# Order of two eviction halves, and other slots for a few steps of the last layer, in a two-layer gated cross-attention kernel

## The chip, the core and the metric

The kernel runs on one core of one Trainium2 chip. The metric is the device time of one execution in microseconds (us). The engines are TensorE (PE in the profile; PEld is its weight load), VectorE (DVE), ScalarE (ACT), GpSimd (POOL) and SyncE (SP, which here only starts DMAs). TensorE writes its products to PSUM, a memory of eight banks here, each of 128 partitions by 512 fp32 numbers; VectorE and ScalarE read a product from its bank and write the result to SBUF, which is called evicting it.

## The reference

Four batches of 512 tokens of width 256 go through two layers, in fp32. Each layer is a cross-attention with 16 heads of width 16, whose keys and values come from the context, and a feed-forward part; each part gets a layer norm of x and is added back through a gate.

```python
x = x + tanh(g_xattn[0]) * attention0(layernorm(x), ctx)      # softmax(q k / 4 - 0.1 |t - t'|) v, then Wo, bo
x = x + tanh(g_ffn[0])   * ffn0(layernorm(x))                 # relu(x W1' + b1) W2' + b2, W' in {-1, 0, 1}
x = x + tanh(g_xattn[1]) * attention1(layernorm(x), ctx)      # q, k, v each through a relu; softmax(q k / 4) v
x = x + tanh(g_ffn[1])   * experts(layernorm(x))              # top-1 of 4 experts, gelu, Wo, bo, inner layer norm
```

In the first feed-forward part the weights are W / (mean |W|) rounded and cut to -1, 0 or 1; the hidden width is 1024 in both.

## The kernel before

**Groups and slots.** The attention of both layers is cut into 32 groups, in the order layer, batch b, half of the heads tt (0 or 1), and e (0 or 1). A projection of width 256 is two halves tt of 128 rows, on which eight heads lie; e tells the even heads from the odd. A group holds four heads, each on 32 partitions of which 16 carry data (the others are zero or hold helper rows). A group has four slots, one for each block of 128 keys (or, for the maxima, of 128 queries), which makes 128 slots u = 0 to 127: layer 0 is slots 0 to 63, layer 1 slots 64 to 127, and batch b of a layer begins at slot 64 * layer + 16 * b. So layer 1's batches 2 and 3 begin at slots 96 and 112.

**A slot.** Function `scores(u)` writes a block of eight matmuls, four heads twice: the scores `pm` of slot u + 6 (LEAD is 6), of which VectorE takes the row maxima (L521), and the transposed scores `psc` of slot u, of which ScalarE takes the exponentials (L536); they come as two groups of four, called quads here. The text calls this block S(u). After it `slot(u)` puts what else is due in that slot:

- `weighted`, in the first slot of a group: the sum `po` of the group before, 16 matmuls on its exponentials and values (L564), copied out by ScalarE (L570);
- `shifted`, in the third: the maxima of the next group transposed to `pmT` (L578) and subtracted from its queries, which makes `q2` (L587 where it is on POOL);
- `divided`, in the third (layer 1, and batch 0 of layer 0): `po` of the group before the last transposed to `pn` (L624), divided by its sums on VectorE and added to x on POOL (for the last group of batches 2 and 3 on VectorE);
- steps from the planner.

**The planner.** `chain(steps, start, end, *after)` takes steps that must follow one another, each with a cost in us and a gap: the step may come no sooner than that many slots after the one before it. A chain begins at slot `start`, after the chains named in `after`, and the last slot of each step is counted back from `end` by the gaps. In a slot the planner takes, among the chains' next steps, the one whose last slot is earliest, and takes it if it is due, if it costs 0, or if it fits in what is left of 3.1 (SLOT) by half its cost. Costs and gaps are the planner's numbers and no waits on the chip. The order in which the program writes instructions is their order on each engine[...].

**The steps that matter here.** `prepare(layer, b)` gives two lists. The first is the norm of the attention's input: `stats` and `more_stats` (each two of `BATCH_NORM_STATS2` and two of `BATCH_NORM_AGGREGATE` on VectorE, L335 and L336, and behind the second a chain of eight small POOL operations), `norm` (four rows on ScalarE, L366) and `turn` (eight transposes into two banks `pt_a`, copied to `xT` by ScalarE, or by ScalarE and VectorE, L382). The second is values: `values(0)` and `values(2)`, each two blocks of the value product `pv` (L430) in one bank. `project(layer, b, tt)` gives `keys` and `queries`: four matmuls (L461) into one bank `pk` or `pq`, and two evictions of that bank, one for each e. In layer 1 ScalarE evicts the half e = 0 (keys L476, queries L498) and VectorE the half e = 1 (L478, L500), and for values ScalarE the first block (L443) and VectorE the second (L445). In layer 0 the queries of batches 2 and 3 are shared in the same manner (L494 on ScalarE, L496 on VectorE); their keys are VectorE's alone (L474).

`ffn0(b)` gives the first feed-forward part of batch b: statistics, norm and transposes (`pt_f`), eight hidden products `ph` (L686) and two residual products `py_f` (L389, 32 matmuls each), which are added to x on VectorE (L394). `route(b)` gives the router's steps of the second (norm, transposes, logits `plg` and, per pair of tokens' blocks, the place of each token, `prk`, `pid`). `quantize` reads the absolute sums of the first feed-forward weights (L281, ScalarE) in the first slots.

**The banks.** All products share one pool: each new product gets the bank that comes free first in the order of the program. A matmul into a bank waits until all readers of what was there before have finished, and a second reader of a bank on another engine comes after the first one in the program.

The calls of the planner for the attention's steps, as they are before the change (L1169 to L1186), and the functions of the evictions follow.

Of the kernel before, what the change touches and what calls it, by code (L numbers as in the profile page):

```python
# [20 lines left out]
B, S, D = 4, 512, 256  # L21
# [20 lines left out]
LEAD = 6  # L42
# [10 lines left out]
def flamingo_kernel(ctx: ExitStack, tc: tile.TileContext, t: dict, out: bass.AP):  # L53
# [11 lines left out]
    def bank_psum(name):  # L65
        return ps.tile([P, 512], F32, tag="bank", name=name)
# [84 lines left out]
    def key_rows(tt, e, eng):  # L151
        kx = wts.tile([P, S], F32, tag="xg", name=f"kx{tt}{e}", bufs=4)
        beta = sml.tile([P, NT], F32, tag="beta", name=f"beta{tt}{e}")
        eng.tensor_scalar(beta, ext[:, e, 1, :], bqk[:, 1, tt, e : e + 1], None, ALU.add)
        for kt in range(NT):
            eng.tensor_scalar(
                kx[:, ts(kt, P)], kpos[:, ts(kt, P)], ext[:, e, 0, kt : kt + 1],
                beta[:, kt : kt + 1], ALU.mult, ALU.add,
            )
        kext[tt, e] = kx  # L160
# [63 lines left out]
    order = const.tile([P, NT, NE], F32, tag="order", name="order")  # L224
# [151 lines left out]
    def transposed(src, dst, name, alone=False):  # L376

        for c in range(NC):
            pt = bank_psum(f"pt_{name}{c}")
            for n in range(NT):  # L380
                nc.tensor.transpose(pt[:, ts(n, P)], src[:, n, ts(c, P)], ident)  # L381
            (nc.scalar.copy if alone or c == 0 else nc.vector.tensor_copy)(dst[:, c, :], pt)  # L382
# [18 lines left out]
    def prepare(layer, b, eng=None, meanwhile=None):  # L401

        nm = f"a{layer}_{b}"
        st = {}

        def stats():
            st["xn"] = act.tile([P, NT, D], F32, tag="xn", name=f"xn_{nm}")
            first, st["more"], st["rows"] = layernorm(
                x[b], st["xn"], 1e-5, nm, eng, meanwhile
            )  # L410
            first()

        def more_stats():
            st["more"]()

        def norm():
            st["rows"]()

        def turn():
            xTs[layer, b] = act.tile([P, NC, S], F32, tag="xT", name=f"xT_{nm}", bufs=2)  # L420
            transposed(st["xn"], xTs[layer, b], nm, layer == 0 and b > 0)

        def values(n0):
            def run():
                wv = attn_w[layer]["wv"]
                vh = v_sb[b % 2][1]
                pv = bank_psum(f"pv{nm}{n0}")
                for n in range(2):
                    for c in range(NC):
                        nc.tensor.matmul(  # L430
                            pv[:, ts(n, D)], lhsT=cT[b][:, c, ts(n0 + n, P)], rhs=wv[:, c, :],
                            start=(c == 0), stop=(c == NC - 1),
                        )
                if layer == 0:
                    nc.scalar.copy(
                        vh[:, n0 : n0 + 2, :, 0:DK], pv.rearrange("p (n h d) -> p n h d", n=2, d=DK)
                    )
                    return
                for n in range(2):
                    to = vh[:, n0 + n, :, 0:DK]  # L440
                    of = pv[:, ts(n, D)].rearrange("p (h d) -> p h d", d=DK)
                    if n == 0:
                        nc.scalar.activation(to, of, AF.Relu)  # L443
                    else:
                        nc.vector.tensor_scalar(to, of, 0.0, None, ALU.max)  # L445

            return run

        return (
            [(stats, 0, 0), (more_stats, 0, 1), (norm, 0, 1), (turn, 0.9, 1)],  # L450
            [(values(0), 1.75, 0), (values(2), 1.75, 0)],
        )

    def project(layer, b, tt):

        nm = f"{layer}_{b}{tt}"

        def product(w, src, name):
            pp = bank_psum(f"{name}{nm}")
            for c in range(NC):  # L460
                nc.tensor.matmul(  # L461
                    pp, lhsT=attn_w[layer][w][:, c, ts(tt, P)], rhs=src[:, c, :],
                    start=(c == 0), stop=(c == NC - 1),
                )
            return pp

        def key_half(pk, e):
            k = act.tile([P, S], F32, tag="k", name=f"k{nm}{e}", bufs=5)
            h = half[:, e : e + 1]
            if (layer, b) == (0, 1):  # L470
                nc.scalar.activation(k, pk, AF.Copy, scale=h)
                nc.gpsimd.tensor_tensor(k, k, kext[tt, e], ALU.add)
            elif layer == 0:
                nc.vector.scalar_tensor_tensor(k, pk, h, kext[tt, e], ALU.mult, ALU.add)  # L474
            elif e == 0:
                nc.scalar.activation(k, pk, AF.Relu, bias=kone[:, e : e + 1], scale=h)  # L476
            else:
                nc.vector.tensor_scalar(k, pk, h, kone[:, e : e + 1], ALU.mult, ALU.max)  # L478
            ks[layer, b, tt, e] = k

        def keys(between=None, halves=range(2)):
            pk = product("wk", cT[b], "pk")
            if between:
                between()
            for e in halves:
                key_half(pk, e)

        def queries():
            pq = product("wq", xTs[layer, b], "pq")
            for e in range(2):  # L490
                q = act.tile([P, S], F32, tag="q", name=f"q{nm}{e}", bufs=4)
                h = half[:, e : e + 1]
                if layer == 0 and (e == 0 or b < 2):
                    nc.scalar.activation(q, pq, AF.Identity, bias=bqk[:, 0, tt, e : e + 1], scale=h)  # L494
                elif layer == 0:
                    nc.vector.tensor_scalar(q, pq, h, bqk[:, 0, tt, e : e + 1], ALU.mult, ALU.add)  # L496
                elif e == 0:
                    nc.scalar.activation(q, pq, AF.Relu, scale=h)  # L498
                else:
                    nc.vector.tensor_scalar(q, pq, h, 0.0, ALU.mult, ALU.max)  # L500
                qs[layer, b, tt, e] = q

        return [(keys, 1.75, 1), (queries, 1.75, 0)]

    def score(out_, lhs, rhs, i, n):
# [640 lines left out]
    def chain(steps, start, end, *after):  # L1146
        last = [end] * len(steps)
        for i in range(len(steps) - 2, -1, -1):
            last[i] = last[i + 1] - max(steps[i + 1][2], 1 if steps[i][1] and steps[i + 1][1] else 0)
        c = dict(steps=list(zip(steps, last)), ready=start, after=after, done=None)  # L1150
        chains.append(c)
        return c

    def first_unit(layer, b):
        return 4 * NT * (B * layer + b)

    ffn = head = None
    ffns = []
    for b in range(B):
        first, rest = ffn0(b)  # L1160
        end = first_unit(1, b) - 15
        head = chain(first, 4 * NT * (b + 1) + 3, 4 * NT * (b + 1) + 9, head)
        ffn = chain(rest, 0, end, head, ffn)
        ffns.append(ffn)
    for layer in range(2):
        for b in range(B):
            u0 = first_unit(layer, b)
            lead, values = prepare(layer, b)
            if (layer, b) == (0, 1):  # L1169
                *early, early_rows, turn_1 = (job for job, *_ in lead)  # L1170
                (early_values, *_), later_values = values
                turned_1 = chain([later_values, (turn_1, 0.9, 1)], 1, 4)
                keys_0, (queries_0, cost, _) = project(layer, b, 0)
                chain([keys_0, (queries_0, cost, 2)], 5, u0 - LEAD - 2, turned_1)
            elif u0:
                chain(
                    [*lead, *project(layer, b, 0)], u0 - 14, u0 - LEAD - 2,
                    ffns[b] if layer else None,
                )
                chain(values, u0 - 8, u0 + 2)  # L1180
            if (layer, b) == (0, 1):
                keys_1, (queries_1, cost, _) = project(layer, b, 1)
                chain([keys_1, (queries_1, cost, 4)], u0 - 5, u0)
            else:
                chain(project(layer, b, 1), max(u0 - 4, 0), u0)
    (totals1, *_), *quant1 = quantize(w1f, "w1", True)  # L1186
# [14 lines left out]
    for b in range(B - 1):  # L1201
        u0 = first_unit(1, b + 1)
# [60 lines left out]
    lead, values = prepare(0, 0, nc.vector, lambda: key_rows(0, 0, nc.vector))  # L1263
    keys, queries = project(0, 0, 0)
# [119 lines left out]
    first = LISTS[2][1]  # L1384
# [131 lines left out]
```

## Time and profile before

| | us |
|---|---|
| median of 3 runs (lowest, highest) | 829.17 (829.14, 830.67) |
| the profiled execution's own time | 829.16 |
| its span, first to last instruction | 827.4 |
| what lies around the span | 1.76 |
| mean granted TensorE clock | 0.997 |

The times and the span are of one core. In the profile a row of instructions names the line, the engine, the operation, output <- input, and the shape; `x512 | 317.0, 682` means 512 instructions, 317.0 us busy in all, 682 ns for one; then comes the engine's idle time just before them and which instruction ended most of it. In the view of waits, a row such as `DVE k L478 <- ACT k L476: 10.0, 8, 1.7` means that VectorE waited at L478 for ScalarE's L476, 10.0 us in all, 8 times, 1.7 us at most. A row of the timeline begins with the start and the duration in us.

A mark for the stages is the start of `po`, which stands in every fourth slot. In the profiled execution the stages between such marks are busy as follows:

| from po of slot | to po of slot | length | PE | DVE | ACT | POOL |
|---|---|---|---|---|---|---|
| (start) | 4 | 50.07 | 45.04 | 38.71 | 24.23 | 27.92 |
| 4 | 24 | 88.66 | 88.43 | 65.63 | 57.94 | 56.34 |
| 24 | 60 | 207.70 | 207.69 | 141.91 | 102.13 | 75.54 |
| 60 | 88 | 157.06 | 156.90 | 108.33 | 86.28 | 32.55 |
| 88 | 112 | 127.00 | 125.21 | 86.56 | 68.55 | 20.28 |
| 112 | (700 us) | 69.51 | 68.53 | 41.65 | 46.87 | 24.73 |
| (700 us) | (end) | 127.40 | 116.67 | 80.77 | 46.39 | 57.69 |

A matmul that waits counts as busy here from the time its engine takes it up, so that PE is shown busy nearly always; how long a block takes from its start to the next one's start tells more. The marks within the fifth stage are po of slot 88 at 503.49, 92 at 528.68, 96 at 556.17, 100 at 571.82, 104 at 592.38, 108 at 610.91 and 112 at 630.49.

### The profile page before, as it was taken

How to read it: one execution, taken by the hardware profiler on the slowest of the kernel's cores; microseconds unless marked ns; L12 is line 12 of the kernel's file. 1: busy time of each engine (PE TensorE's matmuls, PEld its weight loads, DVE VectorE, ACT ScalarE, POOL GpSimd, SP SyncE). 2: the span in 40 equal slices, each digit the busy share in tenths (PEclk: the TensorE clock that was granted, in tenths of full speed). 3: DMA queues.
4: the chain of work that ended last, by engine and by line, in shares of the span. 5: the costliest groups of instructions: out<-in, count | busy, mean ns of one | idle time of the engine just before them, and what ended most of it. 6: DMA issues, size and time to landing. Idle time of an engine off the chain costs nothing. (4 is left out here: it accounts for less than half of the span.)

```text
span 827.4 us, 13610 instructions
## 1 busy us (share of the span) xinstructions
PE 808.5 (98%) x5226; PEld 451.6 (55%) x5226; DVE 563.6 (68%) x1254; ACT 432.4 (52%) x904; POOL 295.0 (36%) x457
## 2 busy tenths in 40 slices
PE   7999999999999999999999999999999999999995
PEld 3544444545464355643465444564444555899994
DVE  6867778766857676567855676557688764799443
ACT  2586665643645453455535566346756666533341
POOL 5658555524233253331011132002314421735622
PEclk9999999999999999999999999999999999999998
DMA  8200000000001000000000001000104322726820
GB/s 316 75 1 1 1 2 1 1 1 1 1 1 39 1 1 1 1 27 1 1 1 1 27 1 52 1 1 1 52 1 153 95 87 78 286 75 245 304 81 32
DMA packets 17712, 42.28 MB, mean 51 GB/s; under 512 B 2032, under 2 KB 12016, under 8 KB 15216
## 3 DMA queue, kind: packets, MB, share of 16 engines
q0 software_dynamic: 5104, 27.34, 9.3%
q1 hardware_dynamic: 12128, 13.54, 4.8%
q8 instruction: 41, 0.67, 0.3%
q10 hardware_dynamic: 416, 0.54, 0.2%
q14 instruction: 23, 0.19, 0.1%
HBM read 35.13 MB, written 6.29 MB: 50 GB/s over the span
## 5 line engine op out<-in xcount | busy, mean ns | idle before, releaser
L521 DVE TENSOR_REDUCE m<-pm 128x1 f32<-128x512 f32 x512 | 317.0, 682 | 109.6 <-PE psc L507 105.2
L536 ACT ACTIVATE p<-psc 128x512 f32<-128x512 f32 x512 | 266.9, 602 | 144.9 <-PE psc L507 142.8
L507 PE MATMUL psc<-q,k 32*128 32x512 f32 x1024 | 274.7, 622 | 0.0
L507 PE MATMUL pm<-k,q 32*128 32x512 f32 x1024 | 261.0, 615 | 1.7 <-ACT q L494 0.9
L539 POOL TENSOR_TENSOR p<-p,dec 128x256 f32<-128x256 f32 x128 | 93.9, 739 | 162.8 <-ACT p L536 162.8
L507 PEld LDWEIGHTS pm<-k,q 32*128 32x128 f32 x1024 | 91.9, 184 | 81.9 <-issue 45.8
L507 PEld LDWEIGHTS psc<-q,k 32*128 32x128 f32 x1024 | 106.0, 183 | 51.7 <-issue 27.4
L564 PE MATMUL po<-p,v 128*32 128x512 f32 x1024 | 116.5, 595 | 0.8 <-DVE m L521 0.8
L564 PEld LDWEIGHTS po<-p,v 128*32 128x32 f32 x1024 | 31.4, 109 | 80.9 <-issue 58.9
L1108 PE MATMUL pg<-xs,wg 128*128 128x128 f32 x608 | 71.6, 276 | 0.7 <-DVE m L521 0.7
L1108 PEld LDWEIGHTS pg<-xs,wg 128*128 128x128 f32 x608 | 69.8, 192 | 4.1 <-DVE m L521 1.7
L587 POOL TENSOR_TENSOR q<-q,mT 128x512 f32<-128x512 f32 x16 | 20.3, 1270 | 132.3 <-ACT mT L586 132.3
L1134 ACT ACTIVATE ha<-pg,wg 128x128 f32<-128x128 f32 x120 | 34.3, 368 | 52.5 <-PE pg L1108 52.5
L686 PE MATMUL ph<-xTf,w1q 128*128 128x512 f32 x128 | 60.0, 605 | 0.0
L570 ACT COPY oT<-po 128x512 f32<-128x512 f32 x32 | 18.7, 585 | 77.0 <-PE po L564 77.0
L1311 PE MATMUL pyf<-wo,ha 128*128 128x256 f32 x256 | 57.6, 379 | 0.0
L389 PE MATMUL py_f<-w2q,h 128*128 128x256 f32 x256 | 57.2, 381 | 0.0
L389 PEld LDWEIGHTS py_f<-w2q,h 128*128 128x128 f32 x256 | 48.0, 190 | 9.3 <-DVE m L521 3.0
L1311 PEld LDWEIGHTS pyf<-wo,ha 128*128 128x128 f32 x256 | 47.6, 190 | 5.9
L686 PEld LDWEIGHTS ph<-xTf,w1q 128*128 128x128 f32 x128 | 22.6, 189 | 30.3 <-issue 18.2
L394 DVE SCALAR_TENSOR_TENSOR x<-py_f,tg,x 128x512 f32<-128x512 f32 x8 | 6.0, 750 | 42.4 <-PE py_f L389 42.4
L461 PE MATMUL pk<-cT,wk 128*128 128x512 f32 x68 | 33.5, 615 | 0.3 <-DMA cT<-in_ctxT_dram 0.3
(263 smaller groups left out, 839.8 us busy)
## 6 DMA issues: line engine op xcount, KB each, us to landing
x<-in_x_dram SPq DMA_DIRECT2D x4, 512.0 KB, 8.4
rows_d<-xn_f SPq DMA_DIRECT2D x4, 512.0 KB, 3.0
rows_d<-x SPq DMA_DIRECT2D x4, 512.0 KB, 3.4
cT<-in_ctxT_dram SPq DMA_DIRECT2D x3, 512.0 KB, 9.5
w1q<-in_w_dram SPq DMA_DIRECT2D x1, 1024.0 KB, 8.9
w2q<-in_w_dram SPq DMA_DIRECT2D x1, 1024.0 KB, 11.2
wo<-in_wo_dram SPq DMA_DIRECT2D x2, 512.0 KB, 3.8
rows<-in_rows_dram SPq DMA_DIRECT2D x1, 640.0 KB, 9.1
```

Of the source, the lines that this page charges most:

```text
L389: nc.tensor.matmul(py[:, n, :], lhsT=operand(c, n0 + n), rhs=w[:, c, :], start=(c == 0), stop=(c == chunks - 1),)
L461: nc.tensor.matmul(pp, lhsT=attn_w[layer][w][:, c, ts(tt, P)], rhs=src[:, c, :], start=(c == 0), stop=(c == NC - 1),)
L507: nc.tensor.matmul(out_, lhsT=lhs[r, ts(n, P)], rhs=rhs[r, :], start=True, stop=True)
L521: nc.vector.tensor_reduce(m[:, n, 2 * pair + i, r : r + 1], pm[i], AX.X, ALU.max)
L536: nc.scalar.activation(p[:, i, :], psc[i], AF.Exp, scale=SCALE)
L539: nc.gpsimd.tensor_tensor(d, d, dec.unsqueeze(1).to_broadcast([P, 2, P]), ALU.mult)
L564: nc.tensor.matmul(po[i * HP : (i + 1) * HP, :], lhsT=v_sb[b % 2][0][:, kt, c0 : c0 + HP], rhs=ps_exp[NT * s + kt, i // 2][:, i % 2, :], s ...
L587: nc.gpsimd.tensor_tensor(q2s[g], qs[g], turned, ALU.subtract)
L686: nc.tensor.matmul(ph, lhsT=w1q[:, c, ts(f, P)], rhs=st["xT"][:, c, :], start=(c == 0), stop=(c == NC - 1),)
L1108: nc.tensor.matmul(ph[:, f, :], lhsT=w[:, c, ts(f2 * NF // 2 + f, P)], rhs=xs[j][:, c, :], start=(c == 0), stop=(c == NC - 1),)
L1134: nc.scalar.activation(ha[:, f, :], (ha if src is None else src)[:, f, :], AF.Gelu, bias=biases[j][:, fa : fa + 1],)
L1311: nc.tensor.matmul(py, lhsT=hs[j, f // 4][:, f % 4, :], rhs=wo1[f // 4][:, f % 4, :], start=(f == 0), stop=(f == NF - 1),)
```

## The change

It has four parts.

1. **The order of two evictions of one bank.** The value halves of layer 1 are written with VectorE's block first, then ScalarE's. The key and query halves are written with e = 1 (VectorE's) first in layer 1 and for batches 2 and 3 of layer 0; batches 0 and 1 of layer 0 keep e = 0 first. Nothing is moved to another engine.
2. **`turn_1`**, the second transposes of batch 1's input in layer 0, has a gap of 2 instead of 1 behind the values ahead of it.
3. **The last layer's last batch**: the first feed-forward part of batch 3 is due two slots earlier (slot 95, not 97); both statistics steps stand in slot 96 (16 before the batch begins), the rest of that chain from slot 97, and its first queries two slots behind its keys, not in the slot they could come in next. The chain of the three outer batches is as before.
4. **Gaps in layer 1**: the second values of batch 2 come six slots or more behind the first; the second queries (tt = 1) of batches 2 and 3 two slots or more behind their keys.

```diff
-                for n in range(2):
+                for n in (1, 0):
                     to = vh[:, n0 + n, :, 0:DK]
                     of = pv[:, ts(n, D)].rearrange("p (h d) -> p h d", d=DK)
...
+        order = (1, 0) if layer == 1 or b > 1 else (0, 1)
+
-        def keys(between=None, halves=range(2)):
+        def keys(between=None, halves=order):
             pk = product("wk", cT[b], "pk")
...
-            for e in range(2):
+            for e in order:
                 q = act.tile([P, S], F32, tag="q", name=f"q{nm}{e}", bufs=4)
...
-        end = first_unit(1, b) - 15
+        end = first_unit(1, b) - (17 if b == B - 1 else 15)
...
-                turned_1 = chain([later_values, (turn_1, 0.9, 1)], 1, 4)
+                turned_1 = chain([later_values, (turn_1, 0.9, 2)], 1, 4)
...
             elif u0:
-                chain(
-                    [*lead, *project(layer, b, 0)], u0 - 14, u0 - LEAD - 2,
-                    ffns[b] if layer else None,
-                )
-                chain(values, u0 - 8, u0 + 2)
+                if (layer, b) == (1, B - 1):
+
+                    (first, *_), (second, *_), *rest = lead
+                    norm = chain([(first, 0, 0), (second, 0, 0)], u0 - 16, u0 - 16, ffns[b])
+                    keys_0, (queries_0, cost, _) = project(layer, b, 0)
+                    chain([*rest, keys_0, (queries_0, cost, 2)], u0 - 15, u0 - LEAD - 2, norm)
+                else:
+                    chain(
+                        [*lead, *project(layer, b, 0)], u0 - 14, u0 - LEAD - 2,
+                        ffns[b] if layer else None,
+                    )
+                if (layer, b) == (1, 2):
+                    values_0, (values_2, cost, _) = values
+                    chain([values_0, (values_2, cost, 6)], u0 - 8, u0 + 2)
+                else:
+                    chain(values, u0 - 8, u0 + 2)
...
+            elif layer == 1 and b > 1:
+                keys_1, (queries_1, cost, _) = project(layer, b, 1)
+                chain([keys_1, (queries_1, cost, 2)], u0 - 4, u0)
             else:
                 chain(project(layer, b, 1), max(u0 - 4, 0), u0)
```

Since the planner fills slots one after the other, steps that the diff doesn't name move as well. In the program as it is built, these are the steps that TensorE has in other slots (the other slots keep theirs):

| slot | before | after |
|---|---|---|
| 2 | pmT, pt_a | pmT |
| 3 | | pt_a |
| 90 | pmT, pn, plg, ph | pmT, pn, pv(0), plg |
| 91 | prk, py_f | ph, prk |
| 93 | pk, pq | py_f |
| 94 | pmT, pn, py_f | pmT, pn, pk |
| 95 | pv(0), pv(2) | py_f |
| 96 | po | po, pq |
| 97 | | pv(2) |
| 98 | pmT, pn | pmT, pn, pt_a |
| 99 | | pk |
| 101 | pt_a | pq |
| 102 | pmT, pn, pk | pmT, pn |
| 103 | pq, pt_f | pt_f |
| 109 | pk, pq | pk |
| 111 | pid | pq, pid |

The order of SyncE's instructions is the same. On POOL the eight small operations of batch 3's norm stand ahead of the query shift and of the addition to x of slot 98.

## The prediction

> **What bounds the kernel now.** I read the page first: its engine totals, then its groups.
>
> ```profile
> PE 808.5 (98%) x5226; PEld 451.6 (55%) x5226; DVE 563.6 (68%) x1254; ACT 432.4 (52%) x904; POOL 295.0 (36%) x457
> ...
> L521 DVE TENSOR_REDUCE m<-pm 128x1 f32<-128x512 f32 x512 | 317.0, 682 | 109.6 <-PE psc L507 105.2
> L536 ACT ACTIVATE p<-psc 128x512 f32<-128x512 f32 x512 | 266.9, 602 | 144.9 <-PE psc L507 142.8
> ```
>
> TensorE (PE) is busy nearly always, and VectorE (DVE) and ScalarE (ACT) wait for its scores (psc). So a step is worth only what it does to PE's order in time. In the timeline of PE a score block S(u) (eight matmuls of slot u) takes 1.93 us from its start to the next block's when nothing holds it; longer ones hold a stall. From the weighted sum po of slot 88 (503.49 us) to that of slot 112 (630.49) the pieces at their shortest sum to 114.5 us (24.3 to slot 92, 56.5 to 104, 17.1 to 108, 16.6 to 112), so 12.5 of the 127.0 us are stall. All that most of the diff can win lies here.
>
> Next the waits, for the evictions whose order is turned round:
>
> ```profile
> DVE k L478 <- ACT k L476: 10.0, 8, 1.7
> DVE v L445 <- ACT v L443: 7.0, 7, 1.4
> DVE q L500 <- ACT q L498: 5.7, 6, 1.5
> PEld psc L507 <- DVE q L500: 3.1, 6, 0.6
> ```
>
> VectorE waits 22.7 us for ScalarE's half, and PE waits for the later half. One such place in the timeline, slots 93 and 94:
>
> ```profile
> 536.21 0.78 ACT L476 ACTIVATE k<-pk,kone,cols 128x512 f32<-128x512 f32 x1 [0.64 <-PE pk L461]
> 537.02 0.81 DVE L478 TENSOR_SCALAR k<-pk,cols,kone 128x512 f32<-128x512 f32 x1 [1.12 <-ACT k L476]
> ...
> 537.92 0.69 ACT L498 ACTIVATE q<-pq,cols 128x512 f32<-128x512 f32 x1 [0.94 <-PE pq L461]
> ...
> 538.71 0.75 DVE L500 TENSOR_SCALAR q<-pq,cols 128x512 f32<-128x512 f32 x1 [0.89 <-ACT q L498]
> ...
> 539.52 1.12 PE L507 MATMUL psc<-q,k 32*128 32x512 f32 x2
> ```
>
> The last pair of S(94) reuses pq's bank: it starts 0.05 us after the second reader ends, and the next block 1.05 later. S(94) takes 2.76 us, 0.83 over.
>
> **The order of the two halves.** Either way the second half starts when the first ends: 0.69 + 0.75 is 0.75 + 0.69. Here a rule of the Trainium skill is weighed (PSUM — Partial Sum Buffer, section PSUM bank collisions raise a hardware error): two engines must not touch one bank at a time, reads included, so a dependency stands between them. The rows above agree, back to back with 0.04 to 0.10 us between. Were the reads free of each other, each of the nine or so blocks that wait for the second half would gain some 0.7, 6 us in all; by row and rule it is 0. The handover from DVE to ACT no row shows; I bound it by 0.1 us either way for each such block (1 us in all), and take 0, as the opposite handover is that short.
>
> The gain is that DVE is free 0.7 earlier, and the cost that ACT's exponentials start some 0.3 later (2.06 for four, 539.12 becoming 539.4). Both are hidden where a long PE piece (po 3.57, py_f 7.1) follows, which is nearly everywhere. Where DVE is late, though, ACT used to read first in its shadow. That is so in layer 0, slots 24 and 40, where four statistics rows stand ahead of DVE's query half:
>
> ```profile
> 226.09 0.81 DVE L496 TENSOR_SCALAR q<-pq,cols,bqk 128x512 f32<-128x512 f32 x1
> ...
> 226.95 1.12 PE L507 MATMUL psc<-q,k 32*128 32x512 f32 x2
> 228.00 1.07 PE L564 MATMUL po<-p,v 128*32 128x512 f32 x8
> ```
>
> In slot 40 the built program now gives that pair a bank that the block's first reduction (0.62) frees: 226.8 + 0.62, so it starts at 227.45, +0.5. In slot 24 it waits for ACT's half after DVE's: 136.5 + 0.75 + 0.75 = 138.05 against 137.38, of which 0.3 was a wait of po for a reduction anyway: +0.35. In slot 79 DVE reaches its value half at 455.25, and ACT's 0.38 comes after: +0.2. Slots 30, 46, 87 and 88 gain about 0.1 each. In slot 107 the +0.4 hides behind DVE's rank of slot 108. **Sum +0.7.**
>
> **turn_1 from slot 2 to slot 3.** The transposes (1.0) leave the place before S(3) and go behind it. But ACT's order matters:
>
> ```profile
> 45.89 1.11 ACT L382 COPY xT_a<-pt_a 128x512 f32<-128x512 f32 x2
> ...
> 48.77 0.71 ACT L281 ACTIVATE abs_w<-w2q 128x512 f32<-128x512 f32 x1
> ```
>
> The copies now stand behind S(3)'s exponentials (46.0 to 48.0) and both absolute sums of slot 3 (1.25): 49.2 to 50.3. S(4)'s third score reuses the bank of the first copy, so it starts at 49.8 and po at 50.85 against 50.07. **+0.8.** If the copies were not waited for, S(4) would end by 49.4: -0.7.
>
> **Slots 88 to 104** (times from po of slot 88; in brackets before). Moved: values(0) 95 to 90, values(2) 95 to 97, the last hidden product 90 to 91, outputs 91 to 93 and 94 to 95, key product 93 to 94, query product 93 to 96; for batch 3 statistics 99 to 96, normalising 100 to 97, transposes 101 to 98, keys 102 to 99, queries 103 to 101. No matmul is added, SP's order is the same, and no DMA is moved; POOL's eight small steps (571.27 to 574.22, 2.95 us) come before the query shift of slot 98, which waits for its copy till later.
> To 92: S(91) is 1.93 (2.77), as the query bank is gone from it; ph waits 0.35 for a reduction, S(92) 0.37 for the rank. PE work 24.3 - 7.08 + 1.83 = 19.05, so po(92) 19.8 (25.19).
> To 96: po 3.57, S 1.93, py_f 7.08, S 1.96, transposes 1.0, pk 1.81, S(95) 2.75 (its last pair waits for k 0.8 and one reduction), py_f 7.0, S 1.96: 29.06, po(96) 48.86 (52.68). With po and pq 5.39 PE is at 54.25, call it T.
> To 100 from T: S(97) 2.55 (waits for q, 0.75 + 0.69), pva 1.83. DVE does q, all four statistics (2.16, by these rows) and only then its reductions, 2.9 to 5.35:
>
> ```profile
> 566.58 0.41 DVE L335 BATCH_NORM_STATS2 st_a<-x 128x6 f32<-128x256 f32 x1
> 567.03 0.18 DVE L336 BATCH_NORM_AGGREGATE mv_a<-st_a 128x2 f32<-128x6 f32 x1
> ...
> 568.37 1.13 PE L507 MATMUL pm<-k,q 32*128 32x512 f32 x4 [0.47 <-DVE m L521]
> ...
> 571.82 0.64 PE L564 MATMUL po<-p,v 128*32 128x512 f32 x4 [0.52 <-DVE m L521]
> ```
>
> v ends on DVE at 5.75, on ACT at 6.2; S(98) waits for it, 4.4 to 7.15. Behind v ACT stands the normalising of batch 3 (ready from POOL at 5.95; 2.07, to 8.27), and behind that S(98)'s exponentials. pt_a needs the bank of their first: 8.85 instead of 8.15, and ends at 9.85. S(99) waits for their last and then for the copies, 2.6, to 12.45; pk 1.82; S(100) 2.58. po(100) at T + 16.85 = 71.1 (68.33).
> To 104: po 3.57, S 1.93, pq 1.82, S(102) 2.58 (q's chain), transposes 1.1, S(103) 2.65 (late reductions behind the other batch's statistics), pt_f 1.45 (normalising to 14.4), S(104) 2.95 (copies behind late exponentials): 18.05 (20.56), po(104) 89.15 (88.89). The stall of the light slots isn't filled: each work put there brings its own eviction. **+0.3**; the two ends of the unknown are below, with the rivals.
>
> **Slots 109 to 112.** The query product goes from 109 to 111. S(110) starts 1.8 earlier, waits for ACT's k (620.08) and ends at 621.15; DVE's selections (1.28 and 0.5) follow its k at 619.26, reductions 620.95 to 623.4; pmT, pn, pidT to 622.8; S(111) waits for the division, to 625.4; pq to 627.2, pid, S(112) waits for q, to 629.9 against 630.49. **-0.6.**
>
> The end of batch 3's chain, the gap in the last layer's second value product and the two-step start of the norm change no more than these moves: 0.
>
> **Sum:** 0.7 + 0.8 + 0.3 - 0.6 = +1.2. Span 827.4 + 1.2 = 828.6; the profiled execution's 829.16 (1.76 around its span, the median of the runs being 829.17) becomes **830.3 us**. I call a difference of 0.2% (1.7 us) what a measurement of this kernel can tell.
>
> **Rival A, ScalarE becomes the bound (slower).** In slots 97 to 104 the normalising stands ahead of exponentials twice, after a POOL chain that starts late. I charge 0.7 and about 1 for them. If POOL's 2.95 or the statistics run later, the whole 2.07 of ACT goes on the path: 2 x 2.07 - 1.7 = +2.4 more, of which 2.0 stays: 832.3. It decides once xn of batch 3 ends later than T + 8.3. For it: ACT has no slack behind v. Against: ACT is 52% busy.
> **Rival B, the light slots are filled (faster).** S(97) to S(100) hold 3.3 us of stall and S(102) to S(104) 2.3. My 89.15 for slots 88 to 104 holds 8.4 of stall over the 80.8 of PE work. If the evictions fit in DVE's idle time and only 5.0 of it is there, the stretch gives -3.1 instead of +0.3: 826.9. For it: DVE is only 68% busy. Against: the rows of slot 99, where PE waits for DVE itself.
> **Rival C, the halves matter more.** If DVE's earlier 0.7 is worth 0.3 in each of eight blocks, -2.4: 827.9; the heavy pieces after them speak against it.
>
> **How the numbers follow.** Forecast 0.42 (829.0 to 831.4 by itself: 0.02 faster, 0.29 same, 0.11 slower): it follows the waits one by one. B 0.25 (0.22 faster, 0.03 same): stalls that I add up one behind the other may overlap. A 0.18 (0.02 same, 0.16 slower); C 0.15 (0.10 faster, 0.05 same). Faster 0.34, same 0.39, slower 0.27. The range takes in A and 0.3 beyond it, and B and 0.9 beyond, since B and a third of C (0.8) can hold together: 826.0 to 832.6.
>
> **What will show it.** po(92), po(96), po(100), po(104), po(112) minus po(88): 19.8, 48.9, 71.1, 89.2, some 126.7. DVE's wait for ACT's k, q and v gone, and ACT waiting for DVE's with S(62), S(72) and S(78) as long as before. po of slot 4 at 50.85; po of slot 40 0.5 later within its own slot. It would be wrong if PE's score blocks in slots 97 to 104 are near 1.93 (B), or if exponentials of slots 98 and 103 start later than I say (A).

## The result and the profile after

The changed kernel takes 831.13 us (median of 15 runs, 831.03 to 833.32) against 829.14 for the kernel before (15 runs): a ratio of 1.0028, interval 1.0021 to 1.0035. It is slower by 2.0 us. The forecast was 830.3, with 826.0 to 832.6 as range.

The profiled execution of the changed kernel took 831.66, with a span of 830.0. Single executions of one kernel differ by a step of about 0.6 or 1.6 us, in the profiles mostly in the first 20 us: `po` of slot 4 starts at 50.07 in the profile of before, at 49.42 in one and at 51.72 in two profiles of kernels with the same code up to there. So what follows compares marks inside the executions, each against the mark ahead of it, and not totals. Summed in this manner the change costs 2.5 us up to `po` of slot 128 in the execution that was profiled, 0.5 more than the medians say. The likely reason is such a step: the changed kernel's times lie at 831.1, 831.7 and 833.3 us, most of them at the first, those of before at 828.5, 829.1 and 830.7, most of them at the second. Matched in this order they differ by 2.5 to 2.7. No execution at 831.1 was profiled, so this is not shown.

The page of the changed kernel, first part and the two groups shown of before:

```profile
PE 812.1 (98%) x5226; PEld 450.1 (54%) x5226; DVE 565.3 (68%) x1254; ACT 429.4 (52%) x904; POOL 294.9 (36%) x457
...
L524 DVE TENSOR_REDUCE m<-pm 128x1 f32<-128x512 f32 x512 | 317.2, 682 | 116.1 <-PE psc L510 112.9
L539 ACT ACTIVATE p<-psc 128x512 f32<-128x512 f32 x512 | 265.4, 602 | 130.9 <-PE psc L510 129.4
```

No instruction is added, and no engine is busier by more than 4 us; VectorE's idle time ahead of the maxima grows from 109.6 to 116.1 us, nearly all of it spent waiting for scores. The waits of the evictions (waiting instruction, releaser, us in all, times, longest) have changed sides:

```profile
ACT v L443 <- DVE v L445: 15.2, 8, 2.8
ACT q L497 <- DVE q L499: 14.1, 4, 3.8
ACT k L476 <- DVE k L478: 12.3, 8, 2.6
ACT q L501 <- DVE q L503: 9.2, 8, 2.2
PEld psc L510 <- ACT q L501: 3.4, 7, 0.6
```

In the rows shown of before VectorE waited 22.7 us for ScalarE's half of keys, values and queries of the last layer; now ScalarE waits 50.8 us for VectorE's, 14.1 of them (L497) for queries of layer 0. Both sums are whole idle times, and part of them passed before the product was there. They alone say nothing about the end: TensorE waits for the second half, whoever reads it (for queries of the last layer 3.1 us in the fourth row of the prediction's waits, 3.4 in the last row here).

Where the time went, by the start of `po` (us against before; "forecast" is the prediction's own term):

| stretch | before | after | difference | forecast |
|---|---|---|---|---|
| to slot 4 (turn_1) | 50.07 | 50.78 | +0.71 | +0.8 |
| slots 20 to 24 (halves, layer 0) | 21.46 | 21.81 | +0.36 | +0.35 |
| slots 36 to 40 (halves, layer 0) | 21.15 | 21.60 | +0.44 | +0.5 |
| other slots up to 88 (halves) | | | -0.07 | -0.2 |
| 88 to 92 | 25.19 | 19.64 | -5.55 | -5.4 |
| 92 to 96 | 27.49 | 29.78 | +2.29 | +1.6 |
| 96 to 100 | 15.65 | 22.57 | +6.93 | +6.6 |
| 100 to 104 | 20.56 | 18.08 | -2.48 | -2.5 |
| 104 to 112 | 38.11 | 37.73 | -0.38 | -0.6 |
| 112 to 128 | 65.55 | 65.83 | +0.28 | 0 |

Three of these places in the timeline (start, duration, instruction). Slot 40: VectorE reaches its query half at 227.16, behind the statistics, and ScalarE, idle for 3.84 us, reads only after it. The block's last pair doesn't wait for that read, which ends at 228.75, but for the bank of VectorE's first maximum, which VectorE can take only behind its half, as forecast.

```profile
227.16 0.78 DVE L499 TENSOR_SCALAR q<-pq,cols,bqk 128x512 f32<-128x512 f32 x1
...
227.97 0.78 ACT L497 ACTIVATE q<-pq,bqk,cols 128x512 f32<-128x512 f32 x1 [3.84 <-DVE q L499]
...
228.59 1.12 PE L510 MATMUL psc<-q,k 32*128 32x512 f32 x2 [0.23 <-DVE m L524]
229.64 0.64 PE L567 MATMUL po<-p,v 128*32 128x512 f32 x4
```

Slots 3 and 4: the two copies of turn_1 stand on ScalarE behind the exponentials and the absolute sums, and half of the next block's transposed scores wait for the first copy's bank.

```profile
49.02 1.13 ACT L382 COPY xT_a<-pt_a 128x512 f32<-128x512 f32 x2
...
49.72 1.13 PE L510 MATMUL psc<-q,k 32*128 32x512 f32 x4 [0.17 <-ACT xT_a L382]
50.78 1.50 PE L567 MATMUL po<-p,v 128*32 128x512 f32 x12
```

Slot 95, the largest miss: VectorE is in the division of the group before (`o`) when the key product is ready, reads it at 542.72, and ScalarE after that. The block S(95) takes 3.23 us where 2.75 were forecast.

```profile
542.38 0.42 DVE L637 TENSOR_TENSOR o<-pn,rec 128x256 f32<-128x256 f32 x1
...
542.72 0.80 DVE L478 TENSOR_SCALAR k<-pk,cols,kone 128x512 f32<-128x512 f32 x1
...
543.55 0.78 ACT L476 ACTIVATE k<-pk,kone,cols 128x512 f32<-128x512 f32 x1 [2.58 <-DVE k L478]
...
545.22 1.13 PE L389 MATMUL py_f<-w2q,h 128*128 128x256 f32 x4
```

### The profile page after: what moved, and what is told of

The parts are those of the page before. It is cut to its first block, busy times and chain, and to the rows that moved or that the text cites. A ratio compares the mean times of both kernels' runs of the same rounds, so it can differ in the third digit from the quotient of the medians.

```text
span 830.0 us, 13609 instructions
## 1 busy us (share of the span) xinstructions
PE 812.1 (98%) x5226; PEld 450.1 (54%) x5226; DVE 565.3 (68%) x1254; ACT 429.4 (52%) x904; POOL 294.9 (36%) x457
## 5 line engine op out<-in xcount | busy, mean ns | idle before, releaser
L524 DVE TENSOR_REDUCE m<-pm 128x1 f32<-128x512 f32 x512 | 317.2, 682 | 116.1 <-PE psc L510 112.9
L510 PE MATMUL psc<-q,k 32*128 32x512 f32 x1024 | 279.1, 622 | 1.0 <-ACT q L497 0.4
```

Source lines behind the costliest of these rows:

```text
L510: nc.tensor.matmul(out_, lhsT=lhs[r, ts(n, P)], rhs=rhs[r, :], start=True, stop=True)
L524: nc.vector.tensor_reduce(m[:, n, 2 * pair + i, r : r + 1], pm[i], AX.X, ALU.max)
```

## The experiments

### The parts by themselves

First the order of the halves alone, on the kernel before:

```diff
-                for n in range(2):
+                for n in (1, 0):
...
+        order = (1, 0) if layer == 1 or b > 1 else (0, 1)
-        def keys(between=None, halves=range(2)):
+        def keys(between=None, halves=order):
...
-            for e in range(2):
+            for e in order:
```

> The kernel before with only the order of the halves turned round (keys, queries and values in layer 1, queries in batches 2 and 3 of layer 0); every step stays in its slot. Theory: the loss is layer 0's alone, where VectorE is late behind the statistics: po of slot 24 +0.36, slot 32 +0.12, slot 40 +0.44, slot 48 +0.11, then -0.3 in layer 1 to slot 88, and nothing in slots 88 to 128: +0.7, 829.9 us. Rival: the turned order also costs where products are evicted in slots 88 to 112 of the last layer, which would account for the 0.9 by which slots 88 to 104 were mis-sized: po(112) minus po(88) 0.5 or more above 127.0, total 830.4 or more.

Measured: 829.96 us, ratio 1.0008 (1.0001 to 1.0015). The marks: slot 24 +0.36, 32 +0.12, 40 +0.44, 48 +0.12, then -0.31 from slot 52 to 88, and in slots 88 to 112 +0.05 (po(112) minus po(88) 127.05). In the slots of before the order is worth nothing in slots 88 to 112, as a sum: S(110) and S(111) grow by 0.81 together, and `pmT` between them shrinks from 1.30 to 0.49. Its loss is layer 0's. The rival falls.

Then turn_1 alone:

```diff
-                turned_1 = chain([later_values, (turn_1, 0.9, 1)], 1, 4)
+                turned_1 = chain([later_values, (turn_1, 0.9, 2)], 1, 4)
```

> The kernel before with only the gap of turn_1 at 2. Theory: the transposes' copies stand behind the exponentials and absolute sums of slot 3, po of slot 4 at 50.78 instead of 50.07, all later marks +0.7: 829.85 us. Rival: the 0.7 is made up by shorter blocks later in the first 24 slots, where the mover leaves a bank free sooner: 829.1.

Measured: 829.87 us, ratio 1.0010 (1.0004 to 1.0017); po of slot 4 at 50.76, and all later marks +0.7. Nothing is made up later.

Then all moved steps of the last layer without the other two: the chain of the last batch, its due slot, and both kinds of gap.

```diff
-        end = first_unit(1, b) - 15
+        end = first_unit(1, b) - (17 if b == B - 1 else 15)
...
+                    norm = chain([(first, 0, 0), (second, 0, 0)], u0 - 16, u0 - 16, ffns[b])
...
+                    chain([*rest, keys_0, (queries_0, cost, 2)], u0 - 15, u0 - LEAD - 2, norm)
...
+                    chain([values_0, (values_2, cost, 6)], u0 - 8, u0 + 2)
...
+                chain([keys_1, (queries_1, cost, 2)], u0 - 4, u0)
```

> The kernel before with all the moved steps of the last layer (the last batch's chain, its end, the gap of the second values, the gaps of the second queries), but the halves in the old order and turn_1 in its old slot. Theory: the moves carry the loss of slots 88 to 104 themselves, since a key or query product in a slot of its own makes the block behind it wait for its two evictions: po(104) minus po(88) 90.0 (before 88.9), po(112) minus po(104) 37.7 (38.1), total 829.9 to 830.2. Rival: the loss there comes from the turned order of the halves in these slots: po(104) minus po(88) 89.2, total 829.0.

Measured: 831.88, ratio 1.0031 (1.0019 to 1.0043). Neither theory nor rival had this. The moves alone cost 2.7 us: po(112) minus po(88) is 129.68, where the changed kernel has 127.80 and the kernel before 127.00. So the three parts don't add up: halves +0.8, turn_1 +0.7 and moves +2.7 make 4.2, and together they cost 2.0 to 2.5. In the moved slots the turned order is worth 1.9 us. The reason is seen on VectorE. In this kernel (moves, old order) the waits in slots 96 to 104 hold these two rows, in which VectorE stands behind ScalarE's read; in the changed kernel it stands there behind the product itself, 4.4 us for the queries and 0.8 for the keys:

```profile
DVE q L500 <- ACT q L498: 5.7, 2, 4.7
...
DVE k L478 <- ACT k L476: 1.6, 1, 1.6
```

In slots 109 and 110 of the same kernel VectorE's list runs late for the same reason:

```profile
621.51 0.81 DVE L478 TENSOR_SCALAR k<-pk,cols,kone 128x512 f32<-128x512 f32 x1 [1.12 <-ACT k L476]
622.24 1.28 DVE L1004 TENSOR_TENSOR sel_d<-from_one,row_d 128x512 f32<-128x512 f32 x2
...
623.99 2.47 DVE L521 TENSOR_REDUCE m<-pm 128x1 f32<-128x512 f32 x4
...
624.72 0.55 PE L624 MATMUL pn<-ident,oT 128*128 128x128 f32 x3 [0.64 <-DVE m L521]
```

In the changed kernel the same key half stands at 621.07 and the maxima at 623.54, although its po(108) is 0.37 later; the pair of transposes there (pmT and pn) takes 0.49 and 0.68 instead of 1.29 and 0.59. The reading is this: in a slot with one product and little else, VectorE's list (eviction, statistics or selections, four maxima of 0.68 each) is longer than TensorE's, so what VectorE waits for ScalarE goes onto the path. Where VectorE itself comes late the order costs instead, as at S(95): 3.23 against 2.84 in this kernel.

### Which of the turned halves it is

The moves, with only the values turned round:

```diff
-                for n in range(2):
+                for n in (1, 0):
                     to = vh[:, n0 + n, :, 0:DK]
```

> The moved steps of the last layer with VectorE's block of the values first, keys and queries in the old order, turn_1 in its old slot. Theory: the order of the values is worth 1.0 of the 1.9 by which the turned order shortened slots 88 to 112 (S(90) 2.40 becomes 2.06, S(98) 2.91 becomes 2.6, pn behind it 1.37 becomes 1.0), keys and queries the rest: total 830.7 to 831.0 against 831.88 with all in the old order. Rival: keys and queries carry it, since their evictions are longer (0.75 against 0.41): total 831.4 or more.

Measured: 831.49, ratio 1.0026 (1.0017 to 1.0034). Slots 88 to 112 take 129.36, 0.3 less than with all in the old order; the rival's side. The block behind pv(0), S(91) by the count of this text (S(90) in the expectation), does go from 2.40 to 2.06, and pn of slot 98 from 1.37 to 0.97, but S(98) becomes 3.32, not 2.6. With keys and queries turned as well S(98) is 2.61, S(102) 2.82 instead of 3.29 and pmT of slot 110 0.49 instead of 1.29, against S(95) 3.23 instead of 2.84. Keys and queries carry 1.6 of the 1.9.

### What the gaps between keys and queries cost

```diff
-                    chain([*rest, keys_0, (queries_0, cost, 2)], u0 - 15, u0 - LEAD - 2, norm)
+                    chain([*rest, keys_0, (queries_0, 0, 0)], u0 - 15, u0 - LEAD - 2, norm)
...
-                chain([keys_1, (queries_1, cost, 2)], u0 - 4, u0)
+                chain([keys_1, (queries_1, 0, 0) if b == 2 else (queries_1, cost, 2)], u0 - 4, u0)
```

> The changed kernel, but the queries of two places beside their keys in one slot, not in a slot of their own: second half of batch 2 (slot 95, before that 94 and 96) and first half of batch 3 (slot 99, before that 99 and 101). Theory: two products in a row cost one wait for the evictions and not two, 0.83 to 1.3 each: po(104) minus po(88) 88.0 to 88.6 instead of 90.07, total 829.2 to 829.8. Rival: the evictions of both products come late together and hold the next block twice as long: po(104) minus po(88) 90 or more, total 831.1 or more.

Measured: 830.03, ratio 1.0011 (1.0003 to 1.0019), 1.1 less than the changed kernel by the medians and 1.65 less by the marks (in this and the next two runs the marks give 0.5 more than the medians, the same 0.5 as in the result). po(104) minus po(88) is 88.42 against 90.07 (before 88.89). The pair in slot 95 carries the gain: S(95) goes from 3.23 to 2.03, S(97) from 2.76 to 1.93 and S(98) from 2.61 to 2.06, and S(96) gets a wait (2.03 to 2.76). The pair in slot 99 gains nothing: S(100) keeps its wait (2.95 to 2.82), and S(102) grows from 2.82 to 3.45 though no product precedes it, since VectorE's maxima of S(101) and its statistics now hold it. So the theory's sum came true (88.0 to 88.6), its total (829.2 to 829.8) narrowly not, and that two products share one wait is shown at one of the two places.

### Whether it is the bank's second reader

In the changed kernel, for batches 2 and 3 of the last layer:

```diff
-                nc.scalar.activation(k, pk, AF.Relu, bias=kone[:, e : e + 1], scale=h)
+                nc.scalar.activation(
+                    k, cT[b][:, 0, :] if b > 1 else pk, AF.Relu, bias=kone[:, e : e + 1], scale=h
+                )
...
-                    nc.scalar.activation(q, pq, AF.Relu, scale=h)
+                    nc.scalar.activation(
+                        q, xTs[layer, b][:, 0, :] if b > 1 else pq, AF.Relu, scale=h
+                    )
```

> The changed kernel, but in the last layer's batches 2 and 3 ScalarE's half of keys and queries is computed from the projection's input in SBUF and not from the product's bank, so that the bank has one reader; the output is not the reference's (half of the heads of these batches get other keys and queries). Theory: the last pair of the block behind a key or query product waits for the bank's second reader: S(97) 2.76, S(100) 2.95, S(102) 2.82, S(110) 2.84 each become 2.0 to 2.3, S(95) 3.23 becomes 2.5; a part is given back where the blocks behind then wait for VectorE's maxima; total 828.6 to 829.9 us. Rival: VectorE's maxima hold these pairs and the second reader only comes beside them: the blocks stay within 0.15, total 830.9 to 831.3.

Measured: 828.36, ratio 0.9988 (0.9981 to 0.9995): 2.8 less than the changed kernel (3.3 by the marks). S(97) 2.04, S(100) 2.03, S(102) 2.64, S(110) 2.03, S(112) 2.01, S(95) 2.64; slots 84 to 88 lose 1.4. Three places show what comes next when the reader is gone: S(91) grows from 2.06 to 2.62, S(98) from 2.61 to 3.32 and pmT of slot 110 from 0.49 to 1.30, since TensorE now runs into VectorE's maxima sooner. Of 5.2 us taken off the blocks 2.2 came back. The second reader is shown as the cause of the wait, with VectorE right behind it. One doubt is left here: ScalarE, which no longer waits for VectorE's read, is also free sooner for its exponentials. The kernel with one reader, below, settles it: there ScalarE's half again starts only after VectorE's instruction, and the blocks are free all the same.

### Whether ScalarE's normalising holds anything

```diff
         def rows_(dst=dst):
+            if name in ("a1_3", "f1_2"):
+                nc.scalar.activation(
+                    dst.rearrange("p n d -> p (n d)"), src.rearrange("p n d -> p (n d)"),
+                    AF.Identity, bias=off[:, 0:1], scale=rstd[:, 0:1],
+                )
+                return
             for n in range(NT):
```

> The changed kernel, but ScalarE normalises batch 3's attention input and batch 2's router input in one instruction over all four rows (with the first row's statistics, so the output is not the reference's) and not in four: about 1.1 us less in slots 98 and 103. Theory of ScalarE on the path: pt_a's wait for an exponential (0.37) and pt_f's for the normalised rows (0.5) go, S(98) to S(104) lose 0.8 to 1.6 in sum, total 829.5 to 830.3. Rival: these blocks wait for VectorE's maxima anyway, po(104) minus po(96) stays within 0.4 of 40.65, total 830.7 to 831.2.

Measured: 829.74, ratio 1.0002 (0.9994 to 1.0011), 1.4 less than the changed kernel (1.9 by the marks). The one instruction takes 1.24 us where the four took 2.08, 0.84 less and not 1.1. Slots 96 to 100 lose 0.84 (pn 0.97 to 0.44, pt_a 1.07 to 0.97, S(99) 2.41 to 2.20). Batch 2's router stands in slot 117, not in 103 as the expectation says: slots 116 to 120 lose another 0.82, and slots 100 to 104 stay as they were. So at both places all that was taken off the normalising came off the path, and at slot 98 it costs at least 0.8, where the prediction charged 0.7; what the other 1.24 us cost was not tried, nor was its charge for slots 103 and 104. The last 0.27 of the 1.9 is slot 126, which is taken up below.

### Kernels that follow from it

The paired products of the run above, the old order in layer 0 and turn_1 in its old slot:

```diff
-        order = (1, 0) if layer == 1 or b > 1 else (0, 1)
+        order = (1, 0) if layer == 1 else (0, 1)
...
-                turned_1 = chain([later_values, (turn_1, 0.9, 2)], 1, 4)
+                turned_1 = chain([later_values, (turn_1, 0.9, 1)], 1, 4)
```

> The changed kernel with the two pairs of products in one slot each, the old order of the halves in layer 0 (turned only in the last layer), and turn_1 in its old slot. Theory: the single terms add up: slots 0 to 88 -0.3, 88 to 104 -0.5, 104 to 112 -0.4, 0.27 back in slot 126: 828.3 us, faster than the kernel before by 0.8. Rival: the terms depend on how the banks fall and don't add: 829.1 or more.

Measured: 827.96, ratio 0.9984 (0.9978 to 0.9991), 1.2 us faster than before and 0.3 below the theory. The terms add up: to slot 88 -0.3, 88 to 104 -0.5, 104 to 112 -0.4, and slot 126 does not take its 0.27.

The next kernel takes the second reader away from every key and query bank of batches 1 to 3 of the last layer, and computes the full result:

```diff
+            if layer == 1 and b > 0:
+                if name == "pk":
+                    raws[b, tt] = act.tile([P, 2, S], F32, tag="blocks", name=f"raw{nm}", bufs=1)
+                raw = raws[b, tt][:, 0 if name == "pk" else 1]
+                nc.vector.tensor_copy(raw, pp)
+                return raw
             return pp
...
-                nc.vector.tensor_scalar(k, pk, h, kone[:, e : e + 1], ALU.mult, ALU.max)
+                (nc.gpsimd if b else nc.vector).tensor_scalar(k, pk, h, kone[:, e : e + 1], ALU.mult, ALU.max)
...
-                    nc.vector.tensor_scalar(q, pq, h, 0.0, ALU.mult, ALU.max)
+                    (nc.gpsimd if b else nc.vector).tensor_scalar(q, pq, h, 0.0, ALU.mult, ALU.max)
```

> The combined kernel of the run before, in which for batches 1 to 3 of the last layer VectorE copies a key or query product once into SBUF, and from there ScalarE makes the half e = 0 and GpSimd the half e = 1 (GpSimd takes 1.7 for such an operation by the rows of its quantizing), so that each bank has one reader for 0.7 and not two for 1.45; the output is the full one. Theory: the second reader's time on the path goes at eight blocks (S(72), S(78), S(87), S(88), S(96), S(100), S(110), S(112)), 0.3 to 0.7 each with what the maxima give back: 824.3 to 826.3 us against 827.96. Rival: VectorE's maxima hold the blocks as soon as the reader is gone, or GpSimd's half comes too late for the maxima six slots on: 827.5 or more.

Measured: 829.06 beside 830.24 for the kernel before on the same chip, ratio 0.9977 (0.9967 to 0.9987). S(72), S(78), S(96), S(100) and S(112) fall to 1.93, the length of a free block, and S(87) to 1.97; S(110), which the theory counted with them, grows from 2.84 to 3.30, since the product behind it, pmT, waits 1.26 us for VectorE's maxima. And S(88) takes 6.09 instead of 2.36:

```profile
501.44 2.00 POOL L511 TENSOR_SCALAR q<-raw,cols 128x512 f32<-128x512 f32 x1
503.47 0.59 ACT L382 COPY xTf<-pt_f 128x512 f32<-128x512 f32 x1 [1.93 <-POOL q L511]
...
504.11 2.17 PE L518 MATMUL psc<-q,k 32*128 32x512 f32 x4 [1.63 <-ACT xTf L382]
...
506.21 5.80 PE L575 MATMUL po<-p,v 128*32 128x512 f32 x32
```

The copy `raw` takes an SBUF tile in turn with the router's transposed rows `xTf`; these wait for GpSimd's half, the banks of `pt_f` wait for them, and the scores for the banks. That is not the whole of the 6.09. In this execution TensorE's granted clock is 0.51 in the mean from 503.7 to 510.7 us, a fall that begins within the 1.63 us without a matmul: the four scores take 2.10 to the start of po where 1.05 is usual, and po takes 5.73 to the next block instead of 3.57, 3.2 us in all. So the collision itself costs about 2.7, and the clock 3.2 more. A further 1.65 went in the first 20 us (see the end). Without both, 831.22 would be 826.4, and two of the twelve runs did take 826.43. That the gap brought the lower clock about is not shown.

With two readers kept at this one place (the first half of batch 2):

```diff
+        one_reader = layer == 1 and b > 0 and (b, tt) != (2, 0)
-            if layer == 1 and b > 0:
+            if one_reader:
```

> As the kernel with one reader, but the first half of batch 2 of the last layer (slots 86 and 87) keeps two readers, since there the SBUF tile that holds the copy is also the one into which the router's transposed rows are copied in slot 88, which made S(88) wait for GpSimd's 2.0 us half (6.09 instead of 2.36). Theory: with that collision gone the rest stands: slots 68 to 80 -1.4, 92 to 100 -1.8, 108 to 112 -0.3 against the combined kernel (827.96): 824.3 to 824.9 us. Rival: GpSimd's halves and the tile's next use collide at other places too: 826 or more.

Measured: 824.53 beside 829.21 for the kernel before on the same chip, ratio 0.9937 (0.9924 to 0.9949), 4.7 us faster; against the combined kernel slots 68 to 80 lose 1.4, 92 to 100 1.8 and 108 to 112 0.25, as the theory has it. The query eviction of slot 99 and the start of po behind S(100), in this kernel and then in the combined one:

```profile
569.52 0.69 DVE L472 COPY raw<-pq 128x512 f32<-128x512 f32 x1 [0.93 <-PE pq L464]
...
570.31 0.72 ACT L510 ACTIVATE q<-raw,cols 128x512 f32<-128x512 f32 x1 [0.87 <-DVE raw L472]
...
570.77 1.99 POOL L512 TENSOR_SCALAR q<-raw,cols 128x512 f32<-128x512 f32 x1
...
571.35 3.64 PE L576 MATMUL po<-p,v 128*32 128x512 f32 x32
```

```profile
571.37 0.75 DVE L503 TENSOR_SCALAR q<-pq,cols 128x512 f32<-128x512 f32 x1 [0.98 <-PE pq L461]
...
572.22 0.69 ACT L501 ACTIVATE q<-pq,cols 128x512 f32<-128x512 f32 x1 [1.01 <-DVE q L503]
...
572.96 1.12 PE L510 MATMUL psc<-q,k 32*128 32x512 f32 x2
...
574.01 1.06 PE L567 MATMUL po<-p,v 128*32 128x512 f32 x8
```

In the first, po starts 1.14 us after the copy ends; ScalarE's and GpSimd's halves run beside it. In the second, ScalarE's read ends at 572.91, the last pair follows 0.05 later, and po starts 1.89 after VectorE's read ended. In both ScalarE starts 0.10 after VectorE's instruction ends, and that one takes nearly as long (0.69 and 0.75); but S(100) takes 1.93 in the first and 2.82 in the second. What differs for the bank is the second reader.

### The changed kernel once more

> The changed kernel once more, since its profiled execution (831.66) lay 0.5 above the median of its runs (831.13). Theory: the marks from po of slot 20 on are the same in every execution but for one step in the first 20 us; the marks' differences to the kernel before are again 0.36 for slots 20 to 24, 0.44 for 36 to 40, 0.80 for 88 to 112; median 831.1 to 831.7. Rival: the 0.5 lies in slots 88 to 128, where then another sum would stand: 88 to 112 within 0.3.

Measured: 832.35 beside 830.24 on the same chip, ratio 1.0024 (1.0016 to 1.0031). The marks from slot 4 to 112 are those of the first profile within 0.04 us (20 to 24 +0.36, 36 to 40 +0.45, 88 to 112 127.79). But this execution has a step of 0.56 in slots 112 to 116, where the first had none: so steps between executions are not only in the first 20 us, against the theory.

## Why the prediction held, and where it didn't

The total came out in the range, but above the forecast: the prediction took 1.7 us as what a measurement can tell, and by that the 2.0 us are slower, to which it gave 0.27, less than the 0.39 for no difference.

**What bounds the kernel** held: TensorE's order in time sets the end, and the differences are found in its score blocks and the transposes behind them.

**The order of the halves, sum +0.7:** +0.73 up to slot 88 in the changed kernel. Its two main places are right: slot 40 +0.44 (forecast 0.5), slot 24 +0.36 (0.35). That the sum is right as well is in part luck. S(30), S(46) and S(87), which were to become 0.1 shorter each, became 0.12 longer; slot 79's +0.2 did not come to the mark, since the block behind it shortened by as much; and S(56), S(63) and S(72) became 0.1 to 0.2 shorter, which was not forecast. The dependency weighed there shows in the rows: ScalarE's read starts 0.03 to 0.10 after VectorE's ends, as short as the opposite handover, so the zero taken for it was right.

**The step that failed is in the same part:** "both are hidden where a long PE piece follows, which is nearly everywhere". That is so in the slots of before (halves alone, +0.05 in slots 88 to 112), but the change itself takes the long pieces away from behind the evictions. There the order is worth 1.9 us, near what rival C gave it (2.4), though rival C didn't see that it takes the moved slots for that. The walk through slots 88 to 112 was made with VectorE first, so its sum contains this gain; what was wrong is to whom it was credited. As "moves" they were given -0.3 in these slots; the runs give the moves alone +2.7 and the turned order on top -1.9.

**turn_1, +0.8:** measured +0.71, by the wait for the copy's bank that was named; po of slot 4 at 50.78 against 50.85.

**Slots 88 to 104, +0.3:** measured +1.2. The pieces: to 92 19.64 (19.8), to 96 29.78 (29.06), to 100 from T 17.09 (16.85), to 104 18.08 (18.05). The mis-sized term is S(95): the forecast 2.75 let VectorE read the key product as soon as it was there, while in fact it was still in a division, and the block took 3.23. That is half of the 0.9, and the rest is at most 0.2 in each of a few pieces.

**Slots 109 to 112, -0.6:** measured -0.4, of which the moved query product alone is +0.4 and the order -0.8.

**Slots 113 to 128, nothing:** +0.27 in S(126). The exponentials of slot 125 start 0.28 later against the scores they follow, in three of the profiles (both of the changed kernel, and the paired one) and in no other. Why is open.

**Rivals.** A (ScalarE as bound): batch 3's normalising ended at T + 8.2, just short of the T + 8.3 beyond which A would decide, and slots 96 to 104 took 0.3 more than forecast from T on, not 2.4. So A falls, but normalising is on the path at the two places tried; what holds most blocks is the pair of readers, and then VectorE. B (light slots filled): wrong; S(97) to S(104) stayed at 2.4 to 2.95 except S(101), which was 1.93.

**The size.** The sum fell short by 1.3 of the 2.5 in the profiled execution: 0.9 in slots 88 to 104, 0.2 in 109 to 112, 0.27 in slot 126.

## What to carry to other kernels

When two engines evict one bank, count both reads as one wait of whoever gets the bank next, and ask which of the two engines has the longer list behind it: that one reads first, but only where it comes free no later than the other. Moving work into light slots doesn't fill them if each piece brings its own eviction; two products side by side shared one wait at one of two places, and one copy to SBUF, with the halves made from there by engines that have time, removed it (VectorE's maxima then held one of the six blocks named). Parts of a change to a schedule need not add up: test each part alone and in the company of the others, and compare marks inside the trace, since 0.5 us of a total can be a step of the execution.

## What was not expected of the hardware

Executions of one kernel differ by steps of fixed size rather than by noise: -0.6 and +1.65 us before po of slot 4 in four profiles of four kernels, against the other profiles with the same code up to there. The row behind the small step is the first normalising, whose four statistics rows on VectorE begin with 0.90 us in the profile of before and with 0.43 in that of the combined kernel; why is open. The large step is TensorE's clock. In both profiles that have it (values first, and the first kernel with one reader) the granted clock is 0.53 in the mean from 12.4 to 15.9 us, where it is 1.00 in the profile of before, and the first query product takes 3.65 us instead of 1.98. TensorE had no matmul for 1.16 and 1.05 us shortly before; but it had none for 1.11 in the profile of before, without a fall of the clock, so that gap alone doesn't decide it. GpSimd's half of a key or query took about 2.0 us (once 2.96) where 1.7 was estimated from its quantizing rows; that was hidden except at slot 88.
